# Fusing each block chunk by chunk ahead of its use, with early weights and one-tensor column operations

## The chip, the cores and the metric

The kernel runs on one core of one Trainium2 chip. The metric is the device time of one execution in microseconds. A core has a matrix engine (PE, with its weight loads shown apart as PEld), a vector engine (DVE), an activation engine (ACT), a general engine (POOL, also called GpSimd) and a queue that issues the DMA transfers (SP). Each takes its own instructions strictly in the order of the program, and they wait for one another through semaphores. All numbers here are float32.

## What is computed

The input is eight samples of 512 channels by 48 x 48 = 2304 positions (L). The reference does two layers, each of which adds its result to the input after a group norm (32 groups of 16 channels):

```python
x = x + attention(_gn(x), Wq, bq, Wkv, bkv)        # layer 0: causal linear attention, 8 heads
x = x + mamba_blocks(_gn(x), ...)                  # layer 1
```

Layer 1 splits the 512 channels into four groups of 128 and runs one state-space block per group, each fed with the fused result of the one before:

```python
prev = None
for i in range(4):
    x_i = spx[i] + prev if prev is not None else spx[i]
    x_m = mamba(x_i, weights[i])           # in-projection, conv of 4 taps, silu, scan over 16 states, gate, out-projection
    fused_global = max(x_i, x_m)
    w_local  = sigmoid(mean(x_i))          # one number per sample and channel, over all positions
    w_global = sigmoid(mean(fused_global))
    fused = w_local * x_i + w_global * fused_global
    prev = fused                           # and it is this group's output
```

The means run over all positions, so the fused values of a block can't be formed before its last position is through.

## The kernel before

Attention and state-space blocks run side by side. Attention goes in *parts* of 384 positions by 128 channels; six parts make one pass over a sample's channel group, and the last part of a pass ends with a `group_norm` of one column (`n == 1`) for that group. A group norm of four columns (`n == 4`) belongs to the statistics of a whole sample's input.

Layer 1 is cut into *blocks* (sample and channel group, 32 in all) and each block into six *chunks* of 384 positions. One chunk of one block is a *job*, 192 in all. Two `Stream` objects take the even and the odd samples; the list `turns` writes out by hand how their jobs alternate, so that between the last job of a block and the first of the next block of the same stream two jobs of the other stream stand. A job has eight *slots*; a slot is two of the sixteen states in both halves of a quarter of the channels and holds four scans on DVE (L816), each fed by a decay on ACT (L805, in PSUM) and by products on DVE (L795, operand in PSUM) and POOL (L784). POOL then weights the scanned values (L832), PE sums them up (L839), and twice a job DVE multiplies the sum by the gate (L851), at slot 2 of the next job and at slot 6 of its own.

The order of the program is made by a small planner in the kernel. It runs slot by slot, and in each slot calls `beside` twice, at *half slots* counted by `half_no`. `beside` advances tasks, which are Python generators: a `yield "n", banks` asks to be resumed n half slots after the last step, when so many PSUM banks are free; `yield (h, 1), 0` asks for half slot h at the earliest. Nothing of this exists on the chip: there, only the resulting order counts. `save` puts a store in a list that `flush` issues on SP two half slots later.

What the change touches:

- `group_norm` (L171 to L191): the mean and the variance of groups through two small matmuls, and between them DVE operations on tiles of one or four columns. L176, L177, L178, L188 and L191 each take two tensors in SBUF.
- `Stream.weights` and `Stream.scale_weights`: the loads of a block's weights, issued by `move_on` when the stream goes to its next block; then an exponential of `av` on ACT (L490), four products of `wk` with `wi` on POOL (L493) and a negation of `av` on POOL (L494). All weight tiles have one buffer per stream. `Job.prepare` waits for `st.scaled`.
- `Stream.pass_on`: the fusion. It starts when the last chunk of a block is through (`finale`), forms the weights `wt` and the sum of the next input (L549, L552), and then goes through the six chunks, one step per half slot: two scalings on ACT (L579, L580), the normalized input of the next group on ACT (L584), then on POOL the addition that makes the fused value (L589), the next block's input (L594) and the output (L597), which is stored. The loads of the following chunk are issued between the ACT and the POOL steps. `self.ready` tells the planner how many chunks of the new input exist; `prepare` of a job begins at most 11 slots (`LEAD`) ahead of the job.

Of the kernel before, what the change touches and what calls it, by code (L numbers as in the profile page):

```python
# [9 lines left out]
F32 = mybir.dt.float32  # L10
AF = mybir.ActivationFunctionType
ALU = mybir.AluOpType
# [4 lines left out]
P = 128  # L17
# [32 lines left out]
def attention_then_mamba_kernel(  # L50
# [17 lines left out]
    nc = tc.nc  # L68
    B, _, L = x.shape
    NS = 16  # L70
# [91 lines left out]
    def group_norm(stats, n, name, bufs):  # L162


        bank = Banks()
        yield "1", 1
        mv = small.tile([P, n, 2], F32, tag=f"mv{n}", name=f"mv_{name}", bufs=1)
        for ct in range(n):
            nc.vector.bn_aggr(mv[:, ct, :], stats[:, ct].rearrange("p c s -> p (c s)"))
        mean_ps = bank()  # L170
        nc.tensor.matmul(mean_ps[:, 0:n], grp, mv[:, :, 0], start=True, stop=True)  # L171
        yield "1", 0
        gm = small.tile([P, 3, n], F32, tag=f"gm{n}", name=f"gm_{name}", bufs=1)
        nc.vector.tensor_copy(gm[:, 0, :], mean_ps[:, 0:n])
        bank.free()
        nc.vector.tensor_sub(gm[:, 1, :], mv[:, :, 0], gm[:, 0, :])  # L176
        nc.vector.tensor_mul(gm[:, 2, :], gm[:, 1, :], gm[:, 1, :])  # L177
        nc.vector.tensor_add(gm[:, 2, :], gm[:, 2, :], mv[:, :, 1])  # L178
        yield "0", 1
        var_ps = bank()  # L180
        nc.tensor.matmul(var_ps[:, 0:n], grp, gm[:, 2, :], start=True, stop=True)
        yield "1", 0
        nc.vector.tensor_scalar_add(gm[:, 2, :], var_ps[:, 0:n], 1e-5)
        bank.free()
        norm = small.tile([P, 3, n], F32, tag=f"norm{n}", name=f"norm_{name}", bufs=bufs)
        nc.gpsimd.tensor_tensor(norm[:, 0, :], gm[:, 2, :], power[:, 0:n], ALU.pow)
        yield "1", 0
        nc.vector.scalar_tensor_tensor(  # L188
            norm[:, 1, :], gm[:, 0, :], -1.0, norm[:, 0, :], ALU.mult, ALU.mult
        )  # L190
        nc.vector.scalar_tensor_tensor(  # L191
            norm[:, 2, :], gm[:, 1, :], float(L), norm[:, 0, :], ALU.mult, ALU.mult
        )
        return norm


# [255 lines left out]
    class Stream:  # L452


        def __init__(self, z, samples):
            self.z, self.samples = z, samples
            self.xi = cpool.tile([P, 3 + L], F32, name=f"xi_{z}")
            nc.gpsimd.memset(self.xi[:, 0:3], 0.0)
            self.b = None
            self.block = -1  # L460
            self.ready = 0

        def weights(self):

            n, z, s = self.n, self.z, self.s
            wi = wpool.tile([P, 512], F32, tag=f"wi{z}", name=f"wi_{n}")
            nc.sync.dma_start(out=wi, in_=win[s])

            wk = wpool.tile([P, 4, 256], F32, tag=f"wk{z}", name=f"wk_{n}")
            nc.sync.dma_start(  # L470
                out=wk.rearrange("p k d -> p (k d)"), in_=wconv[s].to_broadcast([P, 1024])
            )
            wo = wpool.tile([P, 2, P], F32, tag=f"wo{z}", name=f"wo_{n}")
            nc.sync.dma_start(out=wo, in_=wout[s])
            wx = wpool.tile([P, 2, 40], F32, tag=f"wx{z}", name=f"wx_{n}")
            nc.sync.dma_start(out=wx, in_=wxp[s])
            wd = wpool.tile([64, 256], F32, tag=f"wd{z}", name=f"wd_{n}")
            nc.sync.dma_start(out=wd[32:40, :], in_=wdt[s])
            nc.sync.dma_start(out=wd[40:41, :], in_=bdt[s])
            pv = wpool.tile([P, 4], F32, tag=f"pv{z}", name=f"pv_{n}")  # L480
            nc.sync.dma_start(out=pv[:, 0:2], in_=bconv[s])
            nc.sync.dma_start(out=pv[:, 2:4], in_=dskip[s])
            av = wpool.tile([P, 4, NS // 2], F32, tag=f"av{z}", name=f"av_{n}")
            nc.sync.dma_start(out=av, in_=alog[s])
            self.w = wi, wk, wo, wx, wd, pv, av

        def scale_weights(self):
            wi, wk, wo, wx, wd, pv, av = self.w
            yield "2", 0
            nc.scalar.activation(av, av, AF.Exp)  # L490
            for k in range(4):
                yield "1", 0
                nc.gpsimd.tensor_tensor(wk[:, k, :], wk[:, k, :], wi[:, 0:256], ALU.mult)  # L493
            nc.gpsimd.tensor_scalar_mul(av, av, -1.0)  # L494
            self.scaled = True

        def move_on(self):

            if self.b is not None and self.s < 3:
                self.s += 1  # L500
                self.fresh = False
            else:
                self.b, self.s = self.samples.pop(0), 0
                self.fresh = True
            self.ready = 0
            self.block += 1
            self.n = f"{self.b}_{self.s}"
            self.state = small.tile(
                [P, 2, NS // 2, 2], F32, tag=f"state{self.z}", name=f"state_{self.n}", bufs=1
            )  # L510
            self.fsum = small.tile([P, NC], F32, tag=f"fsum{self.z}", name=f"fsum_{self.n}", bufs=1)
            self.fm = dpool.tile([P, L], F32, tag="fm", name=f"fm_{self.n}")
            self.weights()
            self.scaled = False
            tasks.append(Task(self.scale_weights()))

        def pass_on(self):

# [24 lines left out]
            if not last:  # L543
                if self.fresh:
                    self.sums = norm[:, 2, :]
                else:

                    sums = small.tile([P, 2], F32, tag="sums", name=f"sums_{self.n}", bufs=3)
                    nc.vector.scalar_tensor_tensor(  # L549
                        sums[:, 0:1], wt[:, 2:3], wt[:, 0:1], norm[:, 2, :], ALU.mult, ALU.add  # L550
                    )
                    nc.vector.scalar_tensor_tensor(  # L552
                        sums[:, 1:2], wt[:, 3:4], wt[:, 1:2], sums[:, 0:1], ALU.mult, ALU.add
                    )
                    self.sums = sums[:, 1:2]
# [14 lines left out]
            now = loads(0)  # L570
            for c in range(NC):

                yield "1", 0
                cols, icols = slice(c * LC, (c + 1) * LC), slice(3 + c * LC, 3 + (c + 1) * LC)
                fu, xb, xa = now
                if not last:
                    normed = dict(bias=norm[:, 1, :], scale=norm[:, 0, :])
                if old is not None:
                    nc.scalar.activation(fu, fu, AF.Copy, scale=wt[:, 1:2])  # L579
                    nc.scalar.activation(xi[:, icols], xi[:, icols], AF.Copy, scale=wt[:, 0:1])  # L580
                if old is None:
                    nc.scalar.activation(xi[:, icols], xb, AF.Identity, **normed)
                elif not last and not self.fresh:
                    nc.scalar.activation(xb, xb, AF.Identity, **normed)  # L584
                if old is not None:
                    yield "1", 0
                    if c + 1 < NC:
                        now = loads(c + 1)
                    nc.gpsimd.tensor_tensor(fu, fu, xi[:, icols], ALU.add)  # L589
                    yield "1", 0  # L590
                    if not last and self.fresh:
                        nc.scalar.activation(xi[:, icols], xb, AF.Identity, **normed)
                    elif not last:
                        nc.gpsimd.tensor_tensor(xi[:, icols], xb, fu, ALU.add)  # L594
                    self.ready = c + 1
                    yield "1", 0
                    nc.gpsimd.tensor_tensor(xa, xa, fu, ALU.add)  # L597
                    save(out[old[0], old[1] * P : (old[1] + 1) * P, cols], xa)
                else:
                    yield "1", 0  # L600
                    if c + 1 < NC:
                        now = loads(c + 1)
                self.ready = c + 1

    class Job:
# [6 lines left out]
        def prepare(self):  # L612
# [81 lines left out]
                nc.scalar.activation(delta[:, h, :], vps[h], AF.Softplus)  # L694
            bank.free(2, late=True)
            yield "2", 0

            def spread(what):
                s = dpool.tile([256, LC], F32, tag="dscr", name=f"{what}_{n}", bufs=6)
# [190 lines left out]
    while min(count) < total:  # L890
        z = 0 if len(jobs) < ALONE else turns[(len(jobs) - ALONE) % len(turns)]
        if count[z] == total:
            z = 1 - z
        jobs.append(Job(streams[z], count[z], len(jobs) * SLOTS))
        count[z] += 1
    slots = SLOTS * len(jobs)

# [198 lines left out]
    with tc.manual_schedule():  # L1096
        half_no[0] = FIRST - 6
        for st in streams:
            tasks.append(Task(st.pass_on()))
        Task(statistics(0)).finish()  # L1100
        for half in range(FIRST - 6, 0):
# [74 lines left out]
```

## Time and profile before

| | |
|---|---|
| median of 3 runs | 9815.3 us (9814.16 to 9816.18) |
| span of the profiled run | 9811.4 us |
| first scan | 201.8 us after the span's start |
| last scan | 9778.5 us |
| POOL: weighting L832 | 1536 of 3176 ns |
| POOL: product L784 | 1536 of 1272 ns |
| fusion on POOL: L589, L594, L597 | 192, 144, 192 of 1000 ns |
| fusion on ACT: L579, L580, L584 | 192 of 613, 192 of 605, 144 of 697 ns |
| weight scaling: L493, L494 | 128 of 728, 32 of 294 ns |

The page gives for each engine the busy time and its share of the span; for each group of like instructions the count, the busy time, the mean of one, and the idle time of the engine just ahead of them with what ended it. The stretch table gives the same busy times between borders of one's choice. A wait inside an instruction, after it has started, is not idle time: it shows as a longer instruction.

### The profile page before, as it was taken

What the parts mean: (1) busy time and instruction counts of PE and PEld (TensorE: products, weight loads), DVE (VectorE), ACT (ScalarE), POOL (GpSimd) and SP (SyncE); (2) the same over time, 40 slices, a digit from 0 to 9 for tenths busy, and PEclk for the clock granted to TensorE, in tenths of its full rate; (3) what the DMA queues carried; (4) which work ended last, traced back from release to release, by engine and by line L of the source; (5) the groups of instructions that cost most, each with busy time, mean ns of one, the idle gap of its engine ahead of it and who ended that gap; (6) DMA issues with size and microseconds to landing.
All of it is one profiled execution on the core that took longest, in us unless ns stands there. A gap on an engine that the chain in (4) does not pass through costs nothing.

```text
span 9811.4 us, 120393 instructions
## 1 busy us (share of the span) xinstructions
PE 8005.0 (82%) x35714; PEld 3805.1 (39%) x35714; DVE 8465.1 (86%) x11624; ACT 6630.3 (68%) x12624; POOL 8108.8 (83%) x5667
## 2 busy tenths in 40 slices
PE   7888888878888888887888888888888888888865
PEld 4433433333333334333333333433333433334322
DVE  4888888889888888888988888888888888888888
ACT  3666676666776667666677666666666676666666
POOL 3788888888888888888888888888888888888899
PEclk9999999999999999988999999998899999999987
DMA  6566566666666555666666665557666656655555
GB/s 199 154 164 165 160 165 168 171 171 183 175 170 171 160 161 158 169 172 183 177 170 172 167 166 161 161 159 184 179 182 167 165 163 167 170 160 156 163 151 138
DMA packets 1002897, 1642.82 MB, mean 167 GB/s; under 512 B 138592, under 2 KB 797312, under 8 KB 1002240
## 3 DMA queue, kind: packets, MB, share of 16 engines
q1 hardware_dynamic: 1002240, 1635.13, 60.9%
q8 instruction: 282, 4.62, 0.2%
q14 instruction: 375, 3.07, 0.1%
HBM read 1309.06 MB, written 325.58 MB: 167 GB/s over the span
## 4 chain that ended last, share of the span: by engine, by line
DVE 31%; PE 23%; ACT 15%; POOL 11%; issue 9%; DMA 9%; SPq 2%; POOLq 0%; DVEq 0%; ACTq 0%
DVE u L816 20%; PE bank L279 10%; POOL u L832 6%; ACT bank L805 6%; PE yp L839 5%; DVE u L795 5%; PE bank L624 2%; DMA dxr<-xscr 2%; ACT L694 2%; POOL u L784 2%; DMA C<-scr 2%; SPq L724 1%; PE bank L635 1%; PE bank L409 1%; ACT L659 1%
## 5 line engine op out<-in xcount | busy, mean ns | idle before, releaser
L816 DVE TENSOR_TENSOR_SCAN u<-bank,u 128x385 f32<-128x385 f32 (+1 forms) x6144 | 5508.1, 941 | 270.2 <-ACT bank L805 268.6
L832 POOL TENSOR_TENSOR u<-u,C 128x1536 f32<-128x1536 f32 x1536 | 4878.7, 3176 | 463.6 <-DVE u L816 283.7
L805 ACT ACTIVATE bank<-dr,av 128x385 f32<-128x385 f32 (+1 forms) x6144 | 3441.7, 580 | 1618.9 <-DVE u L816 1235.1
L839 PE MATMUL yp<-u,cst 128*64 128x384 f32 x12288 | 2486.2, 527 | 493.7 <-ACT yp L773 264.9
L784 POOL TENSOR_TENSOR u<-B,dxr 128x512 f32<-128x512 f32 x1536 | 1954.2, 1272 | 39.1 <-PE yp L839 24.4
L279 PE MATMUL bank<-xn,wq_sb 128*128 128x384 f32 x4608 | 1908.5, 565 | 20.2 <-DVE fg L868 10.7
L795 DVE TENSOR_TENSOR u<-B,dxp 128x1024 f32<-128x1024 f32 x1536 | 1838.9, 1197 | 13.9 <-ACT dxp L768 11.8
L839 PEld LDWEIGHTS yp<-u,cst 128*64 128x64 f32 x12288 | 797.6, 142 | 1632.2 <-issue 1078.7
L624 PE MATMUL bank<-xi,wk 128*128 128x384 f32 x3072 | 1191.4, 534 | 210.7 <-DVE u L816 162.7
L279 PEld LDWEIGHTS bank<-xn,wq_sb 128*128 128x128 f32 x4608 | 982.3, 224 | 759.3 <-issue 258.7
L830 POOL COPY state<-u 128x4 f32<-128x4 f32 x1280 | 240.9, 188 | 932.0 <-DVE u L816 846.7
L624 PEld LDWEIGHTS bank<-xi,wk 128*128 128x128 f32 x3072 | 603.0, 207 | 854.3 <-DVE u L816 336.7
L291 ACT ACTIVATE ex<-bank,bqkv_sb 128x384 f32<-128x384 f32 x384 | 222.9, 580 | 757.4 <-PE bank L279 738.6
L409 PE MATMUL bank<-cst,rdb 128*128 128x128 f32 x576 | 157.3, 405 | 593.0 <-ACT delta L694 588.9
L851 DVE TENSOR_TENSOR yz<-yp,sz 128x384 f32<-128x384 f32 x384 | 213.3, 556 | 372.6 <-PE yp L839 372.4
L805 ACT ACT_TABLE_LOAD x382 | 490.1, 1283 | 6.7
L732 POOL TENSOR_TENSOR delta<-delta,xs 128x384 f32<-128x384 f32 x384 | 384.1, 1000 | 105.9 <-DMA dscr<-delta 84.4
L635 PE MATMUL bank<-xi,wi 128*128 128x384 f32 x768 | 339.5, 532 | 152.8 <-ACT xs L659 152.8
L392 DVE TENSOR_TENSOR S<-S,bank 128x64 f32<-128x64 f32 x512 | 112.8, 220 | 321.0 <-ACT sz L664 155.6
L348 ACT ACTIVATE vT<-bank,bqkv_sb 128x384 f32<-128x384 f32 x192 | 111.4, 580 | 403.0 <-PE bank L279 403.0
L409 PEld LDWEIGHTS bank<-cst,rdb 128*128 128x128 f32 x576 | 89.1, 196 | 712.9 <-ACT delta L694 684.5
L857 PE MATMUL bank<-yz,wo 128*128 128x384 f32 x768 | 322.6, 542 | 29.2 <-DVE yz L851 12.0
(112 smaller groups left out, 8328.7 us busy)
## 6 DMA issues: line engine op xcount, KB each, us to landing
B<-scr SPq DMA_DIRECT2D x1536, 192.0 KB
C<-scr SPq DMA_DIRECT2D x1536, 192.0 KB
xn<-xn SPq DMA_DIRECT2D x192, 768.0 KB
dr<-dscr SPq DMA_DIRECT2D x768, 192.0 KB
dxr<-xscr SPq DMA_DIRECT2D x768, 192.0 KB
dscr<-delta SPq DMA_DIRECT2D x192, 384.0 KB
xscr<-delta SPq DMA_DIRECT2D x192, 384.0 KB
xn<-in_x SPq DMA_DIRECT2D x48, 768.0 KB
```

The lines of the kernel that those rows point to most:

```text
L279: nc.tensor.matmul(ps, wq_sb[:, kt, j * 512 + o * P : j * 512 + (o + 1) * P], xn[:, kt, :], start=(kt == 0), stop=(kt == 3),)
L409: nc.tensor.transpose(rb[:, i, :], rdb[:, 2 * i : 2 * i + 2, :].rearrange("p e d -> p (e d)"), ident)
L624: nc.tensor.matmul(xc, wk[:, k, h * P : (h + 1) * P], xi[:, c0 + k : c0 + k + LC], start=(k == 0), stop=(k == 3),)
L635: nc.tensor.matmul(zp, wi[:, 256 + h * P : 256 + (h + 1) * P], xi[:, c0 + 3 : c0 + 3 + LC], start=True, stop=True,)
L732: nc.gpsimd.tensor_tensor(delta[:, h, :], delta[:, h, :], xs[:, h, :], ALU.mult)
L784: nc.gpsimd.tensor_tensor(u[:, :, :, 1 + LC - TAIL :], self.B[s % 4][:, :, cols].unsqueeze(2).to_broadcast(shape), self.dxr[s // 4][:, :, ...
L795: nc.vector.tensor_mul(u[:, :, :, 1 : 1 + LC - TAIL], self.B[s % 4][:, :, cols].unsqueeze(2).to_broadcast(shape), self.dxp.unsqueeze(1).to ...
L805: nc.scalar.activation(dA[:, cols], self.dr[h][:, g, cols], AF.Exp, scale=self.w[6][:, 2 * h + g, q + j : q + j + 1],)
L816: nc.vector.tensor_tensor_scan(u[:, j, g, cols], dA[:, cols], u[:, j, g, cols], 0.0, ALU.mult, ALU.add,)
L832: nc.gpsimd.tensor_tensor(h, h, self.C[s % 4].unsqueeze(2).to_broadcast([P, NG, 2, LC]), ALU.mult)
L839: nc.tensor.matmul(self.yp[g * 64 : g * 64 + 64, 0:LC], pair_sum, u[:, j, g, 1:], start=False, stop=(s % 4 == 3 and j == NG - 1), skip_gro ...
L857: nc.tensor.matmul(self.xm[:, 0:LC], self.w[2][:, h, :], self.yz[:, h, :], start=(h == 0), stop=(h == 1),)
```

## The change

Three edits go together. The column operations of the group norm and of the fusion sum are rewritten so that, for one column, no DVE instruction takes two tensors from SBUF: the second tensor is read from PSUM or given as a per-partition scalar. The weights of the next block are loaded and scaled by a task of their own, started in the last chunk's `prepare` of the block before, with a second buffer for the tiles that this block still needs (`wo`, `pv`, `av`). And the fusion no longer runs through all six chunks at once: chunk 0 is fused at the block's change, each further chunk is loaded 36 half slots and fused 30 half slots ahead of the job that uses it, so that its work stands among that of the jobs in between. After the last block of a stream, where no job follows, chunks are loaded and fused in sequence.

```diff
@@ group_norm
         nc.vector.tensor_copy(gm[:, 0, :], mean_ps[:, 0:n])
+        nc.vector.tensor_sub(gm[:, 1, :], mv[:, :, 0], mean_ps[:, 0:n])
         bank.free()
-        nc.vector.tensor_sub(gm[:, 1, :], mv[:, :, 0], gm[:, 0, :])
-        nc.vector.tensor_mul(gm[:, 2, :], gm[:, 1, :], gm[:, 1, :])
-        nc.vector.tensor_add(gm[:, 2, :], gm[:, 2, :], mv[:, :, 1])
+        if n == 1:
+            nc.vector.tensor_scalar(
+                gm[:, 2, :], gm[:, 1, :], gm[:, 1, :], mv[:, 0, 1:2], ALU.mult, ALU.add
+            )
+        else:
+            nc.vector.tensor_mul(gm[:, 2, :], gm[:, 1, :], gm[:, 1, :])
+            nc.vector.tensor_add(gm[:, 2, :], gm[:, 2, :], mv[:, :, 1])
...
-        nc.vector.scalar_tensor_tensor(
-            norm[:, 1, :], gm[:, 0, :], -1.0, norm[:, 0, :], ALU.mult, ALU.mult
-        )
-        nc.vector.scalar_tensor_tensor(
-            norm[:, 2, :], gm[:, 1, :], float(L), norm[:, 0, :], ALU.mult, ALU.mult
-        )
+        for i, factor in ((0, -1.0), (1, float(L))):
+            for ct in range(n):
+                nc.vector.tensor_scalar(
+                    norm[:, 1 + i, ct : ct + 1],
+                    gm[:, i, ct : ct + 1],
+                    norm[:, 0, ct : ct + 1],
+                    factor,
+                    ALU.mult,
+                    ALU.mult,
+                )
@@ Stream.weights (now a task; s = (self.block + 1) % 4)
-            wo = wpool.tile([P, 2, P], F32, tag=f"wo{z}", name=f"wo_{n}")
+            wo = wpool.tile([P, 2, P], F32, tag=f"wo{z}", name=f"wo_{n}", bufs=2)
...
-        def scale_weights(self):
-            wi, wk, wo, wx, wd, pv, av = self.w
-            yield "2", 0
+            self.coming = wi, wk, wo, wx, wd, pv, av
+            yield "3", 0
             nc.scalar.activation(av, av, AF.Exp)
             for k in range(4):
-                yield "1", 0
+                yield "3", 0
                 nc.gpsimd.tensor_tensor(wk[:, k, :], wk[:, k, :], wi[:, 0:256], ALU.mult)
-            nc.gpsimd.tensor_scalar_mul(av, av, -1.0)
+            nc.scalar.mul(av, av, -1.0)
             self.scaled = True
@@ Stream.move_on
-            self.weights()
-            self.scaled = False
-            tasks.append(Task(self.scale_weights()))
+            self.w = self.coming
@@ Stream.pass_on
-                    nc.vector.scalar_tensor_tensor(
+                    nc.vector.tensor_scalar(
                         sums[:, 0:1], wt[:, 2:3], wt[:, 0:1], norm[:, 2, :], ALU.mult, ALU.add
                     )
...
             for c in range(NC):
-                yield "1", 0
+                if c and not last:
+                    first = 2 * self.jobs[self.block * NC + c].start
+                    yield (first - 36, 1), 0
+                    now = loads(c)
+                    yield (first - 30, 1), 0
+                elif c:
+                    yield "3", 0
+                    now = loads(c)
+                    yield "1", 0
+                else:
+                    yield "1", 0
...
-                    if c + 1 < NC:
-                        now = loads(c + 1)
                     nc.gpsimd.tensor_tensor(fu, fu, xi[:, icols], ALU.add)
@@ Job.prepare, after the step sizes
+            if c == NC - 1 and (st.s < 3 or st.samples):
+                tasks.append(Task(st.weights()))
```

## The prediction

> **What bounds the kernel now.** I read the page's engine totals first, then the groups with their idle time, then the stretch table of single jobs, and last the waits in the slow jobs.
>
> ```profile
> PE 8005.0 (82%) x35714; PEld 3805.1 (39%) x35714; DVE 8465.1 (86%) x11624; ACT 6630.3 (68%) x12624; POOL 8108.8 (83%) x5667
> DVE 31%; PE 23%; ACT 15%; POOL 11%; issue 9%; DMA 9%; SPq 2%; POOLq 0%; DVEq 0%; ACTq 0%
> ```
>
> DVE is the busiest engine and leads the chain of waits; POOL is three points behind. An average hides the rhythm, though. A job is eight slots of four scans, so every 32nd scan (L816) in order of time begins a job. The stretch table, with those starts as borders, shows six consecutive jobs (columns: length, then busy time of PE, PEld, DVE, ACT, POOL, the granted PE clock, DMA):
>
> ```profile
> 3129.40:3176.10 46.70, 39.67 (x189) 19.10 (x187) 42.59 (x58) 32.27 (x59) 39.76 (x29) 0.96 0.64 168
> 3176.10:3223.40 47.30, 40.23 (x189) 19.42 (x187) 42.69 (x58) 33.19 (x65) 38.67 (x27) 0.93 0.54 154
> 3223.40:3271.00 47.60, 40.52 (x187) 19.41 (x183) 42.52 (x58) 33.23 (x65) 38.75 (x27) 0.93 0.59 152
> 3271.00:3322.50 51.50, 42.85 (x193) 20.52 (x191) 45.90 (x67) 33.50 (x65) 37.97 (x20) 0.90 0.54 141
> 3322.50:3374.60 52.10, 39.88 (x172) 19.06 (x169) 44.34 (x64) 31.93 (x67) 45.03 (x36) 0.84 0.68 188
> 3374.60:3429.80 55.20, 46.48 (x201) 21.32 (x201) 43.37 (x59) 43.93 (x82) 50.57 (x39) 0.91 0.64 178
> ```
>
> Three jobs take 47.2 us on average with DVE busy 90% of it: these are DVE's own pace. The next three are 4.3, 4.9 and 8.0 us longer, 17.2 in all, and this repeats through the whole run: each row of three belongs to the change of a block. The first of them holds the group norm (DVE +3.3), the second the start of the fusion, two fused chunks and the weight scaling (POOL +6.4), the third the other four chunks (POOL +12, ACT +11).
>
> The same from all 177 jobs between the head and the last eleven (8904.7 us): a least-squares fit of a job's length to what it holds gives 47.25 us, +4.0 per group norm of one column, +1.95 per fused chunk, +0.48 per bn_stats piece, +0.37 for a fusion start with its weight scaling, and -0.12 per xn normalization (0.66 us of POOL each, so four of them, 2.7 us of POOL in four pieces, cost nothing). That last number carries the forecast: POOL work in small pieces, spread out, hides; in a burst it does not. In the waits of the third slow job the burst is named:
>
> ```profile
> DVE u L816 <- ACT bank L805: 7.9, 4, 5.0
> PE yp L839 <- POOL xo L597: 3.2, 1, 3.2
> ```
>
> The scan waited 7.9 us for decays, because ACT stood behind fusion activations; PE's gathers stood behind a fused output on POOL. In the three plain jobs together the scan waited 1.1 us.
>
> [...]
>
> ```profile
> L188 DVE SCALAR_TENSOR_TENSOR norm_m<-gm_m,norm_m 128x1 f32<-128x1 f32 x32 | 37.9, 1185 | 12.2 <-POOL norm_m L186 12.2
> L177 DVE TENSOR_TENSOR gm_m<-gm_m 128x1 f32<-128x1 f32 x32 | 37.0, 1157 | 1.1
> L549 DVE SCALAR_TENSOR_TENSOR sums<-wt,norm_m 128x1 f32<-128x1 f32 x24 | 23.3, 969 | 0.8
> L178 DVE TENSOR_TENSOR gm_m<-gm_m,mv_m 128x1 f32<-128x1 f32 x32 | 5.1, 160 | 1.1
> L191 DVE SCALAR_TENSOR_TENSOR norm_m<-gm_m,norm_m 128x1 f32<-128x1 f32 x32 | 5.1, 159 | 0.0
> L525 DVE COPY wt<-sums 128x1 f32<-128x1 f32 x24 | 3.6, 149 | 0.0
> ```
>
> L188 and L191 have the same operands' kinds and one element per partition, and take 1185 and 159 ns: about 1 us is waiting, counted as busy[...]. [...] for a single column the copy of L525 never took over 151 ns in 32. So I price a one-column tensor_scalar at 150 ns.
>
> **The change part by part.**
>
> *Group norm, one column (32 times).* L176, 177, 178, 188, 191 cost 241+1157+160+1185+159 = 2902 ns. After: a subtraction with a PSUM operand, one tensor_scalar in place of two instructions, two for the products, 4 x 150 = 600 ns. 2.3 us x 32 = 74 us of DVE. It lies on the path: the fit charges 4.0 us for a group norm whose DVE work is 3.5. The rest (matmuls, the power on POOL) stays.
>
> *Group norm, four columns (8 times).* L188 and L191 (1405+151 ns) become eight at 150 = 1200. The square at n=4 keeps two SBUF inputs and may wait 1 us now where L176 did before: between -3 and +8 us, taken as 0.
>
> *Fusion weights (24 times).* L549 and L552, 969+260 ns, become 300: 0.93 x 24 = 22 us of DVE.
>
> *The fusion chunk by chunk.* Nothing is removed: three POOL additions of 1.00 us and ACT's 0.61+0.61+0.70 per chunk remain. Chunk 0 follows the fusion weights as before; chunk c > 0 loads 36 half slots ahead of its job and fuses 30 ahead. With the job order written in the kernel that puts one chunk into each job instead of two and four into two of six. The additions stand one half slot (3 us) apart. POOL in a plain job goes from 38.7 to about 42.2 us (3.0 of fusion, 0.5 of weight scaling on average) of 47.2, with xn to 44.9. Queued behind each addition is a product (L784) or a weighting (L832); the gated product of DVE (L851) waits for the latter through PE at slots 2 and 6. The additions fall into slots 2 to 3.5, just after one of these and three slots ahead of the other, and POOL idles 8.6 us a job now. ACT's 1.9 us fall inside the cushion of three decays, 3 x 0.94 = 2.8 us of scanning. The cost per chunk is bounded by 0 (what the xn pieces show) and 1.2 us (the 1.95 of the burst less most of its pile-up); I take 0.5. 174 x (1.95-0.5) = 252 us saved.
>
> *Weights early.* The loads go from the block change to the last job of the block before, nine small DMA groups each; they wait for the convolutions and gates of that job, all done when the step size is computed. Four POOL products of 0.73 us come three half slots apart; the negation moves from POOL (294 ns) to ACT (about 230 ns, as the exponential L490). The first job of a block no longer waits for scaled weights, so its convolution stands earlier on PE. Priced at nothing, hidden by the POOL slack above.
>
> *The tail.* Before, the loads of chunk c+1 are queued on SP ahead of the store of chunk c; now they come after it, and SP stands in that store until POOL's last addition. In the timeline of the end: load issued 9786.95, ACT starts 9789.54, POOL 9790.74, the addition ends 9792.80, store issued by 9793.2. So 6.25 us a chunk in sequence, 6 x 6.25 = 37.5, against 21.5 now (9786.95 to 9808.47): +16 us.
>
> Sum: 9815.3 - 74 - 22 - 252 + 16 = 9483, forecast **9485 us**.
>
> **The rivals.**
>
> *POOL becomes the second bound.* At 42 to 45 us of 47.2 its queue no longer recovers between chunks and products come late: 1.2 us a chunk, 174 x 0.7 = 122 more: 9607. For it: the final jobs, where POOL is at 95%, stretch with every chunk; against it: the jobs with xn, 41.3 us of POOL, take 47.7. Chance 0.2.
>
> *The whole excess goes.* A chunk costs nothing, as xn: 174 x 0.5 less: 9398. Chance 0.13.
>
> *The burst was not the cause.* The stalls at the block change come from the first convolution squeezed among other PE work, and come back wherever a chunk is fused: only the DVE columns and the tail count, 9815 - 96 + 16 = 9735. Chance 0.06.
>
> *Slower.* Each chunk's three additions delay the products of their job in full, 3.0 us a chunk, since each job now has a delayed slot and none recovers: 174 x 2.5 = 435 over the forecast, 9920. Against it: 8.6 us of POOL idle time per job. Chance 0.04.
>
> **How the numbers follow.** The forecast has 0.57. The range reaches from the full absorption, 9400, to a little over the POOL rival, 9620; it leaves out the last two rivals (0.10) and the edges. Faster: all but the slower case and a sliver of no change: 0.95; same 0.01; slower 0.04.
>
> **What would show it.** Right: job lengths nearly even at 47 to 49.5, no triple of long jobs; the column operations at 150 ns; the scan's wait for decays well under the present 268.6 us; POOL's total near 8100; an end that takes 16 us longer after the last scan. Wrong: a POOL row or a PE wait for POOL (L832, L784) that grows in every job; DVE waits at the gated product above 372.6 us; column operations still near 1 us.

## The result and the profile after

| | median us | lowest to highest | ratio to before |
|---|---|---|---|
| before (on the same chip) | 9814.7 | 9814.0 to 9816.2 | 1 |
| after | 9639.1 | 9637.2 to 9645.1 | 0.9822 [0.9805, 0.9839] |

The change saves 176 us. The forecast was 330 us, a time of 9485: it is 154 us too low, and 9639 lies above its range of 9400 to 9620.

The engine totals and the chain of waits of the page after:

```profile
PE 7872.1 (82%) x35714; PEld 3775.8 (39%) x35714; DVE 8374.0 (87%) x11640; ACT 6607.9 (69%) x12656; POOL 8106.6 (84%) x5635
DVE 34%; PE 23%; ACT 17%; DMA 9%; issue 8%; POOL 5%; SPq 3%; POOLq 0%; DVEq 0%; ACTq 0%
```

DVE has 91 us less to do than the 8465.1 of before. In the chain, POOL fell from 11% to 5%, and ACT rose from 15% to 17%. ACT's own work hardly changed (6630.3 and 6607.9 us), so what changed is where it stands.

The stretch table of six consecutive jobs, again three plain ones and then a block's change (columns: borders, length, busy time of PE, PEld, DVE, ACT, POOL, granted PE clock, DMA share, GB/s):

```profile
3359.32:3408.53 49.21, 40.93 (x189) 19.55 (x187) 42.61 (x59) 33.85 (x62) 41.61 (x30) 0.90 0.61 163
3408.53:3457.08 48.55, 40.23 (x189) 19.40 (x187) 42.67 (x58) 34.72 (x68) 41.57 (x30) 0.93 0.60 166
3457.08:3505.25 48.17, 39.83 (x187) 19.12 (x183) 42.45 (x58) 34.84 (x69) 42.80 (x32) 0.93 0.67 188
3505.25:3554.77 49.52, 40.11 (x193) 19.56 (x191) 43.67 (x66) 34.94 (x69) 42.12 (x25) 0.93 0.57 151
3554.77:3604.28 49.51, 40.69 (x177) 19.56 (x174) 43.84 (x65) 32.24 (x65) 42.37 (x30) 0.90 0.66 181
3604.28:3652.89 48.61, 41.64 (x197) 20.03 (x196) 42.80 (x59) 36.57 (x70) 40.26 (x30) 0.96 0.60 159
```

The saw-tooth is gone: 48.2 to 49.5 us everywhere, where it was 46.7 to 55.2. The six take 293.6 us, against 300.4 in the table of before. The first three rows are the puzzle. A plain job was to take 47.25 us and half a microsecond for its chunk, 47.75. They take 48.6 on average, with DVE's busy time unchanged (42.6, as before) and POOL at 42, as forecast. DVE stands idle longer, and the waits of DVE in three plain jobs say where. The first fence is before, the second after (columns: us in all, times, longest):

```profile
DVE yz L851 <- PE yp L839: 6.7, 3, 2.6
...
DVE q L414 <- PE bank L409: 2.0, 3, 0.7
```

```profile
DVE yz L865 <- PE yp L853: 7.3, 3, 3.0
DVE q L423 <- PE bank L418: 5.8, 3, 1.9
```

`q` is a product of attention that has nothing to do with the change. In each of these jobs it now waits 1.9 us for a transposition on PE (L418) instead of 0.66. PE in its turn waits there for ACT. In the first plain job (of the table in the prediction, and of the one above):

```profile
PE bank L409 <- ACT delta L694: 3.9, 1, 3.9
```

```profile
PE bank L418 <- ACT delta L705: 5.2, 1, 5.2
```

The other waits of PE in these two jobs are the same to a tenth. The tables say what such a wait is worth: take PE's busy time from the length of each plain job, and 7.03, 7.07 and 7.08 us are left before, 8.28, 8.32 and 8.34 after. So what stands beside PE's busy time was the same in all three jobs of before, and it grew by the 1.3 us at L418. The rest of the differences in length is PE's busy time (more on this below).

The groups of the page show the same wait over the whole run, and the two waits that the forecast watched (columns: busy us, mean ns, idle us just before and what ended it):

```profile
L830 DVE TENSOR_TENSOR_SCAN u<-bank,u 128x385 f32<-128x385 f32 (+1 forms) x6144 | 5493.3, 938 | 105.2 <-ACT bank L819 104.4
L865 DVE TENSOR_TENSOR yz<-yp,sz 128x384 f32<-128x384 f32 x384 | 211.8, 552 | 354.5 <-PE yp L853 354.5
L418 PE MATMUL bank<-cst,rdb 128*128 128x128 f32 x576 | 160.0, 411 | 724.7 <-ACT delta L705 693.2
```

The scan's wait for decays fell from 268.6 to 104.4 us and the gated product's from 372.6 to 354.5, both as the forecast wanted. But the transpositions' wait for the step size (`delta`, the softplus at L705) rose from the 588.9 us that the group of L409 has before to 693.2 us.

### The profile page after: what moved, and what is told of

Same layout as the page of the kernel before. It is cut to its first block, busy times and chain, and to the rows that moved or that the text cites. A ratio compares the mean times of both kernels' runs of the same rounds, so it can differ in the third digit from the quotient of the medians.

```text
span 9643.0 us, 120121 instructions
## 1 busy us (share of the span) xinstructions
PE 7872.1 (82%) x35714; PEld 3775.8 (39%) x35714; DVE 8374.0 (87%) x11640; ACT 6607.9 (69%) x12656; POOL 8106.6 (84%) x5635
## 4 chain that ended last, share of the span: by engine, by line
DVE 34%; PE 23%; ACT 17%; DMA 9%; issue 8%; POOL 5%; SPq 3%; POOLq 0%; DVEq 0%; ACTq 0%
DVE u L830 22%; PE bank L288 10%; ACT bank L819 7%; DVE u L809 6%; PE yp L853 4%; DMA B<-scr 4%; POOL u L846 3%; PE bank L635 2%; ACT L705 2%; DMA C<-scr 2%; SPq L738 2%; ACT L819 1%; PE bank L418 1%; PE bank L646 1%; DVE sm L436 1%
## 5 line engine op out<-in xcount | busy, mean ns | idle before, releaser
L830 DVE TENSOR_TENSOR_SCAN u<-bank,u 128x385 f32<-128x385 f32 (+1 forms) x6144 | 5493.3, 938 | 105.2 <-ACT bank L819 104.4
L853 PE MATMUL yp<-u,cst 128*64 128x384 f32 x12288 | 2407.1, 509 | 335.9 <-ACT yp L787 231.5
L288 PE MATMUL bank<-xn,wq_sb 128*128 128x384 f32 x4608 | 1938.9, 572 | 64.9 <-ACT delta L705 62.0
L809 DVE TENSOR_TENSOR u<-B,dxp 128x1024 f32<-128x1024 f32 x1536 | 1834.4, 1194 | 10.6 <-ACT dxp L782 10.6
L288 PEld LDWEIGHTS bank<-xn,wq_sb 128*128 128x128 f32 x4608 | 989.8, 226 | 822.5 <-issue 267.4
L418 PE MATMUL bank<-cst,rdb 128*128 128x128 f32 x576 | 160.0, 411 | 724.7 <-ACT delta L705 693.2
L865 DVE TENSOR_TENSOR yz<-yp,sz 128x384 f32<-128x384 f32 x384 | 211.8, 552 | 354.5 <-PE yp L853 354.5
L418 PEld LDWEIGHTS bank<-cst,rdb 128*128 128x128 f32 x576 | 90.5, 199 | 840.5 <-ACT delta L705 816.2
L694 PE MATMUL bank<-dbc,wd 9*128 9x384 f32 x768 | 310.1, 518 | 53.9 <-ACT dbc L686 52.4
```

Source lines behind the costliest of these rows:

```text
L288: nc.tensor.matmul(ps, wq_sb[:, kt, j * 512 + o * P : j * 512 + (o + 1) * P], xn[:, kt, :], start=(kt == 0), stop=(kt == 3),)
L418: nc.tensor.transpose(rb[:, i, :], rdb[:, 2 * i : 2 * i + 2, :].rearrange("p e d -> p (e d)"), ident)
L809: nc.vector.tensor_mul(u[:, :, :, 1 : 1 + LC - TAIL], self.B[s % 4][:, :, cols].unsqueeze(2).to_broadcast(shape), self.dxp.unsqueeze(1).to ...
L830: nc.vector.tensor_tensor_scan(u[:, j, g, cols], dA[:, cols], u[:, j, g, cols], 0.0, ALU.mult, ALU.add,)
L853: nc.tensor.matmul(self.yp[g * 64 : g * 64 + 64, 0:LC], pair_sum, u[:, j, g, 1:], start=False, stop=(s % 4 == 3 and j == NG - 1), skip_gro ...
```

## The experiments

The sums over the 177 jobs between the head and the last eleven are used throughout: 8904.7 us before and 8718.8 after. "A group" is the mean of six jobs over the 16 groups without a sample's statistics: 300.6 us before, 292.8 after. The forecast's figures give 287.6 (six jobs of 47.25, six chunks of 0.5, and 1.1 that it left for the block's change). Letters in the expectations stand for theories: A, that ACT's scalings stand in a bad place; B, that POOL is the second bound (the rival of the prediction); C, that the first job of a block is prepared too late; D, that what is left at the block's change has other causes.

### Later, and with less POOL or less ACT work

Three variants of after. The first starts the chunks four half slots later:

```diff
-                    yield (first - 30, 1), 0
+                    yield (first - 26, 1), 0
```

> The changed kernel with one number altered: chunks are fused 26 instead of 30 half slots ahead of their job, so that ACT's three scalings stand behind the step sizes (softplus) of the job then in preparation instead of ahead of them. Theory A (ACT order: the 1.9 us of scalings delay the softplus, which frees the PSUM banks that the attention's transposes take, and DVE's product q stands in its queue until then): DVE's wait at q for PE falls from 1.9 to 0.65 us in a plain job, about 1.2 us in some 145 jobs, 9640 - 170 = 9470 us. Theory B (POOL is the second bound; its three additions per job cost 1.2 us wherever they stand): 9640 within 30 us.

Measured: 9728.2 us, 0.9913 [0.9898, 0.9928], 89 us slower than after and far from both expectations. The wait of `q` is back at 0.66 us, as theory A had it. But DVE's scan product now waits for the copy of `dxp` on ACT, 110.2 us in all where it was 10.6 in after, a wait that the forecast had never looked at:

```profile
DVE u L809 <- ACT dxp L782: 110.2, 80, 6.1
```

The place of ACT's scalings does not by itself explain this wait. ACT too stands idle ahead of the copy, for the transfer that brings its input `dxr`: 229.3 us in all, against 6.2 in after. In one plain job (start, duration, line and operation, idle time before; lines between them left out):

```profile
3500.50 0.34 SPq L160 DMA_DIRECT2D out<-xo  x1
...
3503.58 1.25 SPq L725 DMA_DIRECT2D dxr<-xscr  x2
...
3509.61 0.59 ACT L782 COPY dxp<-dxr 128x512 f32<-128x512 f32 x1 [4.99 <-DMA dxr<-xscr]
```

The store of the fused chunk goes out only when POOL's third addition (L612) has ended, at 3500.47, and the loads of a job's inputs stand right behind it on SP. In the median a load of `dxr` now follows 2.8 us behind such a store; in after it was 13.2. So the four half slots cured the one queue and hurt another. This is read from the trace; a variant with the old places of the stores was not tried.

The second leaves out two of the three POOL additions for chunks 1 to 5 (`if c == 0 or last:` ahead of L604 and L612), the third leaves out ACT's scalings for these chunks (the same condition at L595 and L600).

> The changed kernel with two of the three POOL additions (the fused value and the output) left out for chunks 1 to 5 of every block that has a successor; ACT's scalings stay where they are, so the output is not that of the reference. Theory A: 9640 within 25 us, DVE's wait at q unchanged at 1.9 us per plain job. Theory B: two thirds of the 1.2 us per chunk come back, 145 x 0.8 = 116, so 9525 us.

> The changed kernel with ACT's scalings (of the fused term, the old input and the normalized input) left out for chunks 1 to 5 of every block that has a successor; POOL's additions stay, so the output is not that of the reference. Theory A: the 1.2 us per job come back, 9470 us, and DVE's wait at q is 0.65 us per plain job. Theory B: 9640 within 25 us.

Measured: 9630.1 us, 0.9811 [0.9797, 0.9826], without the additions; 9561.4 us, 0.9742 [0.9726, 0.9758], without the scalings. Taking 2 of the 3 us of POOL out of each chunk leaves the sum of the 177 jobs where it was: 8711.9, against 8718.8 in the profiled run of after and 8711.6 in that of e6 below, which is the same program up to its end. The gain of 9 us comes in the last ten jobs (426.6 against 436.0), by which time attention's projections are over (in after the last matmul of L288 starts at 9101.5 us). Taking out ACT's 1.9 us brings the sum to 8638.4, and the wait of `q` to 0.66. So the cost of a chunk in the 177 jobs lies on ACT and not on POOL. But it was half of what theory A had been trusted with: 78 us and not the whole miss.

### The columns alone

Before, with the two column edits and nothing else (the hunks of `group_norm` and of the fusion sum).

> The kernel before with the column operations of the group norm and of the fusion sum alone rewritten as in the change; fusion in a burst and late weights stay. If the wait inside these DVE instructions lies on the path, as the forecast had it, 9815 - 96 = 9719 us. Rival: DVE gives the time back at its next wait for ACT or PE, and the kernel gains less than 40 us, 9775 or more.

Measured: 9720.9 us, 0.9906 [0.9891, 0.9921], 93 us below the 9813.8 of before in the same comparison, with 96 forecast. The groups in the profile after show the operations:

```profile
L195 DVE TENSOR_SCALAR norm_m<-gm_m,norm_m 128x1 f32<-128x1 f32 x64 | 10.4, 205 | 10.2 <-POOL norm_m L191 10.2
L178 DVE TENSOR_SCALAR gm_m<-gm_m,mv_m 128x1 f32<-128x1 f32 x32 | 8.7, 272 | 1.2
L556 DVE TENSOR_SCALAR sums<-wt,norm_m 128x1 f32<-128x1 f32 x24 | 6.5, 273 | 0.9
```

The microsecond inside L177 and L188 of before is gone. The traces show what it went with. Before, L177 of one column began 31 of 32 times while POOL was in a product (L784) and ended 0.01 to 0.03 us after it, as at the block change of the prediction's table (start, duration, line and operation; lines between them left out):

```profile
3303.70 1.26 POOL L784 TENSOR_TENSOR u<-B,dxr 128x512 f32<-128x512 f32 x1
...
3303.80 1.19 DVE L177 TENSOR_TENSOR gm_m<-gm_m 128x1 f32<-128x1 f32 x1
```

The one time POOL was idle it took 160 ns. L549, with two inputs in SBUF too, ended like this behind POOL all 24 times. In after, its successor L556 began each time while POOL was at work and ended 0.4 to 0.7 us ahead of POOL's instruction, after 272 or 273 ns. A column operation with two per-partition scalars takes 272 ns and one with a single such scalar 205 ns, where I priced 150, a small error.

### The same scalings behind the softplus

The timeline of ACT in the first plain job of after, which begins at 3359.32 (columns: start, duration, line and operation, idle time before):

```profile
3362.50 0.60 ACT L596 ACTIVATE fu<-fu,wt 128x384 f32<-128x384 f32 x1
3363.01 0.60 ACT L597 ACTIVATE xi<-xi,wt 128x384 f32<-128x384 f32 x1
3363.51 0.69 ACT L601 ACTIVATE xb<-xb,norm_m 128x384 f32<-128x384 f32 x1
3364.11 0.56 ACT L819 ACTIVATE bank<-dr,av 128x384 f32<-128x384 f32 x1
3364.69 1.28 ACT L705 ACT_TABLE_LOAD   x1
3365.99 0.87 ACT L705 ACTIVATE delta<-bank 128x384 f32<-128x384 f32 x2
```

Three scalings, a decay, and only then the softplus of the job in preparation, ahead of which ACT loads a table for 1.28 us. That softplus reads its input from PSUM banks that the planner gives to attention's transpositions next (L418); PE stands at them until the softplus is done, and `q` on DVE, which takes their result, stands with it. The decays that I had counted as a cushion are in time (the scan waits 1.1 us for them in three plain jobs, before and after). The instruction that was late is not one of theirs.

If this is so, the scalings need not go: they need only stand behind the softplus of the same half slot. The planner takes tasks in order of age; the edit lets the fusion, POOL's additions included, be the last of its half slot:

```diff
-            yield from job.stream.pass_on()
+            tasks.append(Task(job.stream.pass_on(), late=True))
...
-        for t in tasks + heads:
+        for t in sorted(tasks, key=lambda t: t.late) + heads:
```

> The changed kernel with the fusion's steps taken last among the tasks of a half slot: the half slots stay, but ACT's three scalings now stand directly behind the softplus of the job in preparation, and ahead of the table load for the decays, instead of directly ahead of the softplus. If it is their place ahead of the softplus that costs (theory A), DVE's wait at q returns to 0.65 us per plain job and the time falls by the 78 us that leaving the scalings out gave, to 9560. Rival (ACT has no free place, the 1.9 us only move): the decays come 1.9 us later behind the table load, the scan waits for them, and the time stays at 9640 or rises to 9700.

Measured: 9556.1 us, 0.9734 [0.9720, 0.9749]. The sum of the jobs is 8638.4, the same as without the scalings. The timeline of the same job, which here begins at 3330.57:

```profile
3334.68 1.28 ACT L705 ACT_TABLE_LOAD   x1
3335.97 0.87 ACT L705 ACTIVATE delta<-bank 128x384 f32<-128x384 f32 x2
3336.73 0.62 ACT L596 ACTIVATE fu<-fu,wt 128x384 f32<-128x384 f32 x1
3337.23 0.61 ACT L597 ACTIVATE xi<-xi,wt 128x384 f32<-128x384 f32 x1
3337.74 0.70 ACT L601 ACTIVATE xb<-xb,norm_m 128x384 f32<-128x384 f32 x1
```

The table load starts 4.11 us into the job where it was 5.37, and 1.26 us is what `q` waits less, and PE at L418 (5.2 us back to 3.9). The cost of the scalings' place is shown: 73 to 80 us in the 177 jobs (from e6's 8711.6 or after's 8718.8), 0.42 to 0.46 us for each of the 174 chunks in them. Of the 128 us that `q` waits less over the whole run (225.1 to 96.6), a part comes back at other waits of DVE: 26 us at the gated product, 20 at L401.

One more variant of after gives two of the three scalings (L596, L597) to POOL, which makes POOL busier by 2.5 us a chunk (the expectation had reckoned with 1.3):

```diff
-                if old is not None:
+                if old is not None and c and not last:
+                    nc.gpsimd.tensor_scalar(fu, fu, wt[:, 1:2], None, ALU.mult)
+                    nc.gpsimd.tensor_scalar(xi[:, icols], xi[:, icols], wt[:, 0:1], None, ALU.mult)
+                elif old is not None:
```

> The changed kernel with two of the three scalings (the fused term and the old input) of chunks 1 to 5 moved from ACT to POOL, so that POOL has about 1.3 us more and ACT 1.2 us less per chunk. Theory A with POOL still free: two thirds of the 78 us that leaving the scalings out gave, 9640 - 50 = 9590. Rival (POOL at 43.5 to 46 us of 48 per job is now the bound): 9640 or more, up to 9750.

Measured: 9583.2 us, 0.9761 [0.9747, 0.9776], 56 us faster than after, with POOL busy 8456.5 us. This is 350 us of added work on the engine that the rival takes for the bound, and the kernel got faster. The 177 jobs take 8638.6 us, as in e5, though one scaling of 0.7 us still stands ahead of the softplus: that one cost nothing there. The 27 us by which this kernel lies above e5 come in the last ten jobs (454.0 against 430.0), where POOL's work does count. For the 177 jobs the rival falls.

### The end, and the early weights

The tail as the prediction had it: the loads of the next chunk stand behind the last store. In the variant, the final fusion of the stream that ends last loads chunk c + 1 ahead of the additions again:

```diff
+                elif c and self.z:
+                    yield "1", 0
+                    now = nxt
...
+                    if last and self.z and c + 1 < NC:
+                        nxt = loads(c + 1)
```

> The changed kernel with the old order of loads in the very last fusion: the loads of chunk c+1 are queued on SP ahead of the store of chunk c. The stretch from the last job's first scan to the end falls from 83.4 to 67.5 us, and the time by 16 us to 9624. Rival: the stores would have gone out just as late and nothing is gained, within 4 us of 9640.

Measured: 9621.1 us, 0.98 [0.9785, 0.9814]: 18 us come back. The stretch from the last job's first scan to the end is 83.4 us in after, 67.5 before and 67.4 in the variant, a difference of 16.

The second variant loads and scales the weights at the block's change again, as before did:

> The changed kernel with the weights loaded and scaled at the block's change as before (one step per half slot), the fusion still chunk by chunk. If early weights were worth nothing, as the forecast had it, 9640 within 20 us. Rival: the first job of a block waits for its weights again and its convolution is squeezed in late, about 3 us in 29 block changes, 9640 + 90 = 9730.

Measured: 9652.0 us, 0.9833 [0.9816, 0.9849], 13 us slower than after by the medians; the two ratios' intervals overlap, and the 177 jobs of the profiled runs differ by 3 us (8722.0 and 8718.8). The rival's 90 us fall. That part of the change, priced at nothing, is worth at most a little.

### What is left with the scalings out of the way

The version of e5 still lies 158 us above the 9398 that the rival "the whole excess goes" gives. Where? First candidate: the first job of a block is prepared one half slot later than the others, since it waits for chunk 0. The variant sets `self.ready = 1` for chunk 0 ahead of the last POOL additions:

```diff
                     nc.gpsimd.tensor_tensor(fu, fu, xi[:, icols], ALU.add)
+                    if c == 0:
+                        self.ready = 1
```

> The kernel of e5 (scalings behind the softplus) with the first chunk reported ready one half slot earlier, so that a block's first job is prepared 22 half slots ahead like all others, and not 21. Theory C (what is left of the block change is the preparation of the first job in the wrong half slot, which meets attention's steps on PE and ACT: DVE's waits at rd, S and q behind it, about 3 us a block): 9556 - 29 x 3 = 9470 us. Rival D (what is left is DVE's own work and chunk 0's fusion): 9556 within 20 us.

Measured: 9598.7 us, 0.9782 [0.9767, 0.9796], 43 us slower than e5. The job where the fusion starts takes 51.9 us and not 49.0, with the scan waiting 3.3 us for decays in it. Both expectations fell: preparing earlier makes that job longer, not shorter. One of PE's waits over the whole run says why:

```profile
PE bank L637 <- POOL xi L611: 118.9, 24, 5.0
```

L611 is the addition on POOL that makes the new input of chunk 0, and L637 the convolution of the job's preparation, which reads it. Reported ready half a slot earlier, chunk 0 lets the convolution into PE's queue before its input is there, and PE stands for up to 5 us, at 24 of the block changes; in e5 this wait comes to 10.0 us in all. The same edit, together with e5 and the tail of e6:

> All three together: scalings behind the softplus, the first job prepared in the common half slot, the old order of loads in the last fusion. By theory C 9556 - 87 - 18 = 9451 us, by theory D 9538 us; either way faster than the kernel before and the changed one.

Measured: 9584.2 us, 0.9768 [0.9753, 0.9782], which carries the same loss. Second candidate: the scalings of chunk 0, which still stand at the block's change. The variant of e5 leaves them out (`and (c or last)` at L595, `and c` at L600):

> The kernel of e5 with ACT's scalings of chunk 0 left out (chunks 1 to 5 keep theirs), so the output is not that of the reference. Theory C: they cost little, 9556 within 20 us, since the late preparation stays. Theory D: the first chunk's 1.9 us on ACT, in the middle of attention's steps, cost 1.5 us or more a block, 9556 - 45 = 9510 us or less.

Measured: 9557.8 us, 0.974 [0.9724, 0.9756], no difference from e5 (9556.1), so theory D's price for them falls too. Third: POOL's additions once more, now that nothing else is in the way, as in e2 but on e5:

> The kernel of e5 (scalings behind the softplus) with two of the three POOL additions left out for chunks 1 to 5 of every block with a successor; the output is not that of the reference. In e2 the same was done while ACT's delay stood, which may have covered POOL's. If POOL's additions cost about 0.5 us per plain job, 9556 - 50 = 9505 us. If the remainder stays at the block change, 9556 within 20 us.

Measured: 9545.6 us, 0.9727 [0.9712, 0.9741]. The 177 jobs take 8638.4 us again, to the tenth; the gain comes in the last ten jobs, 419.6 us against 430.0. Outside the last ten jobs POOL's additions cost nothing.

The last one decides. It is e5 with chunks 1 to 5 emptied: the conditions of e2 and e3, and L609 left out as well, so that of a chunk that feeds a next block only the loads and the store stay.

> The kernel of e5 with all of ACT's scalings and POOL's additions left out for chunks 1 to 5 of every block with a successor (in the six that begin a sample ACT still writes the new input); loads, stores and the order of everything else stay, and the output is not that of the reference. This is the floor for what the chunks can cost. If the chunks explain the remainder, 9480 us; if it stays at the block change (group norm, fusion weights, chunk 0, the first job's preparation), at most 35 us less than e5, 9520 or more.

Measured: 9535.7 us, 0.9718 [0.9702, 0.9734]. The 177 jobs take 8631.6 us, 7 us from e5. So in e5 a chunk's ACT and POOL work is all but free, 0.04 us a chunk, and still the jobs do not come down to 47.25. The three plain jobs in the stretch table of this kernel (columns as above):

```profile
3323.91:3371.73 47.82, 40.79 (x189) 19.55 (x187) 42.61 (x58) 32.31 (x59) 38.70 (x27) 0.93 0.61 168
3371.73:3419.59 47.86, 40.79 (x189) 19.55 (x187) 42.68 (x59) 33.19 (x65) 38.70 (x27) 0.93 0.62 169
3419.59:3467.41 47.82, 40.77 (x187) 19.43 (x183) 42.46 (x58) 33.31 (x66) 39.85 (x29) 0.93 0.67 189
```

These do the work of the plain jobs of before, with nearly the same busy time of DVE, ACT and POOL, and take 47.8 us each, as do those of e3, e5 and e8. Before, the plain jobs took 46.9, 47.4 and 47.6 us over the 16 groups: rising away from the burst, towards 47.8. In e4, which has the new columns and keeps the burst, they took 46.9, 47.4 and 47.6, so it is not the columns. The wait in which they differ is the gated product's for PE, 1.8 us in the first plain job after a burst, 2.6 in the third, 2.9 in e13.

The tables say what made PE earlier. Here too 7.03, 7.07 and 7.05 us are left when PE's busy time is taken from a job's length, as before. So a plain job is shorter behind a burst by just as much as PE is less busy in it, 39.67 us against 40.79 in the first. That difference lies almost wholly in one group of matmuls, attention's 24 projections of a job (L279 before, L288 here; columns: borders, length, busy time of these matmuls and of their weight loads, granted PE clock, DMA). The first fence is before, the three plain jobs in turn, the second e13:

```profile
3136.03:3154.57 18.54, 9.71 (x24) 4.78 (x24) 0.93 0.53 151
3182.77:3201.83 19.06, 10.23 (x24) 5.09 (x24) 0.91 0.35 100
3230.08:3249.38 19.30, 10.46 (x24) 5.21 (x24) 0.89 0.37 107
```

```profile
3330.55:3350.18 19.63, 10.80 (x24) 5.23 (x24) 0.88 0.37 105
```

The same 24 matmuls take 9.71, 10.23 and 10.46 us behind a burst and 10.8 without one, at a granted clock that falls in the same order, 0.93, 0.91, 0.89 and 0.88. The differences from 10.80 are 1.09, 0.57 and 0.34 us; those of the job lengths from 47.82 are 1.12, 0.52 and 0.22. So the burst of before gave back part of what it took, in the jobs behind it, through PE; 47.25 was not the pace of a job without a burst. Why the clock granted there is higher behind a burst is not shown: PE stands idle for longer in the burst (12.2 us in its second job), but no run varied that alone.

### The two repairs together

e5 and the tail of e6 in one kernel:

> The kernel of e5 with the old order of loads in the last fusion, as in e6: 9556 - 18 = 9538 us, faster than the kernel before and the changed one. Rival: the two overlap and it stays at 9556.

Measured: 9542.9 us, 0.9723 [0.9709, 0.9738]. It is the best kernel that does the whole computation: 96 us faster than after, 270 us faster than the kernel before in the same comparison (9812.7). The stretch from the last job's first scan to the end is 67.5 us, so the 16 us of the tail are all there; the medians of this kernel and e5 differ by 13.

## Why the prediction was wrong

- **The columns**: right. 96 us forecast (74 + 22), 93 measured by themselves in e4. Taken in parts from the rows, the group norm of one column gave 69 us and not 74, the fusion sum 16.5 and not 22 (272 ns in place of 150). The square of the four-column norm, bounded between -3 and +8 us and taken as 0, came out at +5 us after for the four-column norm as a whole. The price, that of a copy (L525, never over 151 ns), was an estimate. That such an operation on one column does not stand until POOL's instruction ends is shown by L556 in after, 24 of 24 times; by what rule L177 and L549 did stand so long, no run tells.
- **POOL's additions**: right, they hide (e2, e12, and e8 with still more on POOL), but for the last ten jobs. The rival's 9607 came within 32 us of the result, and its cause had no part in it: a number that fits is no evidence for the story that it came with.
- **Chunk cost of 0.5 us**: right in size by luck, 0.42 to 0.46 measured, and wrong in kind. I bounded it by what POOL pieces cost and checked ACT's 1.9 us against a cushion of three decays. The scans waited no longer for decays (1.1 us in three plain jobs, before and after); PE waited for the softplus (5.2 us in the first plain job), and DVE for PE (1.9 us at `q`). The question "what is queued behind the waiting instruction on its engine, and who waits for that" was asked of POOL and of the decays, and not of the softplus.
- **The tail**: right, +15.9 us with +16 forecast.
- **The weights early**: priced at 0, worth between 3 us (177 jobs of the profiled runs) and 13 us (medians).
- **The failed step: "174 x 1.95" as what a spread chunk can save.** This term of the sum was 339 us before the 0.5 was taken off. Measured without the scalings' cost, it is the way from e4 (8822.8) to e5 (8638.4): 184 us, or 1.06 us a chunk, with whatever the early weights gave inside. The 155 us between are the miss. Two parts of the fit made it. Its base, 47.25 us, was the mean of jobs that profited from the burst ahead of them (the prediction calls them DVE's own pace; they follow PE's busy time); without a burst the pace is 47.8, and six jobs in each group make this 6 x 0.55 = 3.3 us. And other work at a block's change came in the data only together with chunks, so the fit could not well tell one from the other and gave part of it to the chunks: in e13, without chunk work, a group takes 290.1 us, that is 3.2 over six jobs of 47.82, where the forecast had left 1.1. Together 5.4 us a group, 157 us over some 29 groups. By size this accounts for the miss; the pace is shown by e13, and the split of the rest within a block's change (DVE is busy 43.7, 43.8 and 42.9 us in its three jobs in e13, against 42.6 in a plain one; the rest is waits) is read from its rows and was not tried apart.
- **The same, job by job.** Over the 16 groups, from e4 to e13, the three jobs of the change get 8.8 us shorter and the three plain ones 1.6 us longer: 7.2 us a group, where 6 x 1.95 = 11.7 was counted on. The six include chunk 0, of which the prediction says itself that it stays where it was; what chunk 0 costs there beyond ACT's scalings, which e11 shows free, no run tells. The fit was soft as well: counted again from the trace of before, it gives 47.4 us, 1.8 to 1.9 per chunk and 0.0 per xn normalization, in place of 47.25, 1.95 and -0.12.
- **What would have shown it**: every sign that the prediction named came out on the side of right: even jobs, no triple of long ones, the columns far below 1 us (if not at 150 ns), the scan's wait down, POOL's total the same, the tail. The signs tested the mechanism; none tested the size. The rows of before held the warning, 46.70, 47.30, 47.60: three jobs alike in work that get longer the further they are from the burst, with PE's busy time rising beside them by the same amounts. Once in that run, behind a smaller burst, three plain jobs already took 47.8 (2826.93 to 2970.34). I averaged over all.

## What to carry to other kernels

A wait that repeats in bursts need not be worth its whole height (here the three plain jobs behind it got 1.6 us longer without it): look at the stretches right behind it, and if they are shorter than those farther away, subtract what they gave back; a fit over rows that always come together cannot do that. It helps to subtract each engine's busy time from the length of like stretches: where the rest stays the same, their length follows that engine, here PE, though DVE is the busiest. When work moves to another place of an in-order queue, find the instruction directly behind the new place, ask which buffers it frees and who waits for these, whatever the engine's share of busy time says; and ask the same of the queue of transfers, where a store behind the moved work can hold up the loads of others (in e1 ACT's copy waited 229.3 us for them, 6.2 in after). And among the signs that are to show a forecast right, one should test its size: here the length of a plain job, 48.6 us against the 47.75 of the forecast, told of the miss.

## What the hardware showed

- POOL at 84% to 88% of the span had room for small pieces: taking some 290 us away (8106.6 to 7815.1 in e2) left the 177 jobs as they were, and adding 350 us did so too (e8 against e5); the last ten jobs gained 9 and lost 24 us. ACT at 69% charged 73 to 80 us for 1.9 us a chunk ahead of a softplus, and nothing for 0.7 us there (e8).
- A multiplication of 128x384 values by a per-partition scalar took 1248 ns on POOL (e8) and 600 ns on ACT (after). POOL's normalization of the same size, also a tensor_scalar, took 667 ns (L312 after); what makes the difference stays open.
- Jobs of equal work differed by 0.9 us in the mean (46.9 and 47.8), in step with the busy time of 24 matmuls in each: 9.71 us at a granted clock of 0.93 behind a burst, 10.80 us at 0.88 without one.
- A DVE operation on one column, with both inputs in SBUF, took 1157 ns in the mean and 160 at its shortest (L177 before); the profile counts the microsecond between as busy. In 31 of its 32 runs it began while POOL was in a product and ended 0.01 to 0.03 us after it. The same product with per-partition scalars, and an addition with it, took 272 ns (L178 after).
